# Reordering the filler work of a blocked graph recurrence: last-block tasks after base tasks, VectorE-evicted gates first

## The chip, the cores and the metric

The kernel runs on one core of one Trainium2 chip, in one launch. The metric is the device time of the launch in microseconds. The profile is of one execution whose span is 5644.6 us; times of engines and waits come from it.

## The reference

Four graph layers follow one another on 16 graphs (B) of 1024 nodes (N) with 256 features (D), all in float32. Each layer normalizes, applies ReLU, and adds its result to `x`. Layers 0, 1 and 3 multiply the adjacency matrix with the features. Layer 2, the one that the change touches, is a recurrence over the nodes, in their order:

```python
def step(h, i):
    x = jnp.take(h_e, i, axis=1)
    row = jnp.take(norm_adjT, i, axis=1)
    x_par = jnp.einsum('bj,bjd->bd', row, h)
    iou = x @ W_ioux.T + b_ioux + x_par @ W_iouh.T + b_iouh
    r, z = jnp.split(iou, 2, axis=1)
    r, z = (jax.nn.sigmoid(r), jax.nn.sigmoid(z))
    hc = jnp.tanh(x @ W_coux.T + b_coux + x_par * r @ W_couh.T + b_couh)
    h_new = z * x_par + (1.0 - z) * hc
    h = jax.lax.dynamic_update_slice(h, h_new[:, None, :], (0, i, 0))
    return (h, None)
h_out, _ = jax.lax.scan(step, h_e, jnp.arange(n))
```

A node needs the new rows of those earlier nodes to which it has an edge, and the old rows (`h_e`) of the later ones. About 3% of the edges are there.

## The kernel before

`layers_0_1()`, `layer_2()` and `layer_3()` run one after the other. The rest of this section is about `layer_2()`.

**Blocks and sub-blocks.** The 1024 nodes are 8 blocks (t) of 128, a block is 8 sub-blocks (s) of 16. All 16 graphs go together, in two groups (`G2`) of eight, so that 8 graphs x 16 nodes fill the 128 rows of an instruction. Inside a sub-block the 16 nodes are solved in rounds: three always (`round_`, with `change` ahead of the second and third), and more where a chain of edges inside the sub-block is longer. Whether it is, the program knows from a register: `tc.If(n_more[0][s] > 0)` runs `one_more` (L750), and a loop inside it (L753) runs further ones. The Else arm has no round.

**What enters a sub-block.** The sums over parents come in four parts:

- base tasks (`base_tasks`, L414): for the nodes of the next block, the sums over all rows but those of the block just before them. In block t they work for block t+1 and read the rows of the blocks 0 to t-1 from `hn_d`, the new rows in DRAM, and those from t+1 on from `he_d`, the old ones. A graph's rows are the tile `hb` (two DMAs, L392 and L393), its part of the adjacency is `ab` (L389), masked on GpSimd (L398). A graph takes 7 tasks of two products each, all in one PSUM tile `pf`, which VectorE then scales and writes to `bxt` (L420). `ab` and `hb` have two buffers each.
- last tasks (`last_tasks`, L456): the sums over the rows of the block just before, for all nodes of a block but its first 16. They run in the first sub-block of a block, one task of two products for each graph; the rows are `hr` (L441, from `hn_d`), the adjacency is `ao` (L438), scaled on GpSimd (L452). A pair of graphs shares one `ao` and one `hr`, two buffers each; every task has a `pf` of its own, which VectorE adds to `bxt` (L459).
- far tasks (`far_tasks`, L564): the same inside a block, from one sub-block to the later ones; `next_block` (L551) gives the first 16 nodes of the next block (`pnx`).
- `near` (L772): from a sub-block to the next one.

`pf` has three buffers, shared by base tasks, last tasks, far tasks and gates.

**The order of the work.** TensorE, VectorE, ScalarE and GpSimd are under a manual schedule: their queues are in the order in which the program calls them. A sub-block has a list `todo` of base tasks (14 in each) and of the list `behind`, which is the last tasks in the first sub-block and the far tasks in the others. The two are interleaved, the one with the larger share left going first. The closure `fill(weight)` then issues tasks until the issued cost reaches the given part of the list's cost, at six points of a sub-block: 0.15 ahead of the first round, 0.2 in each of the first two rounds after the pc products (while ScalarE and VectorE finish the round), 0.12 in each `change` after the px products, and the rest in the third round. A task's TensorE work is issued at once, its eviction is put in the list `late` and issued at the next `evict()`.

**Gates.** The input part of the gates for the sub-block ahead is in the class `Gates`: two r tasks (L528, 128x256, evicted by ScalarE at L530) and two z tasks (L536, 128x512, evicted by VectorE at L538). They are four calls in `self.tasks`. In the Else arm they run one after the other, evictions one task behind; in `one_more` they are its fillers: one ahead of the px products, one after them, one after the pc products, the last at the end. `seed_r` (L541) and `seed_zc` (L544, L545) copy the results to the PSUM tiles `pr`, `pc` and `pz`, to which the rounds add.

**DMAs.** Loads are issued by SP, whose queue is ordered by a scheduler by need; a load waits for its buffer there and holds up those behind it. The new rows `h` go out in two stores to `hn_d` from GpSimd's queue (L766) at the end of every sub-block, and only then can `hr` and the rows of the newest block in `hb` be read.

Of the kernel before, what the change touches and what calls it, by code (L numbers as in the profile page):

```python
# [19 lines left out]
DC = D // P  # L20
# [3 lines left out]
G2 = 2  # L24
# [14 lines left out]
def gnn_stack(ctx: ExitStack, tc: tile.TileContext, a: dict, out: bass.AP):  # L39
# [278 lines left out]
    def layer_2():  # L318
        with ExitStack() as st:
# [111 lines left out]
            def last_tasks(t, bxt, dv):  # L431

                n = P - S
                loaded = {}

                def load(b0):
                    ao = big.tile([P, 2, n], F32, name="ao")
                    nc.sync.dma_start(ao, a["adj"][b0 : b0 + 2, (t - 1) * P : t * P, t * P + S : (t + 1) * P]  # L438
                                      .rearrange("b p i -> p b i"))
                    hr = big.tile([P, 2, D], F32, name="hr")  # L440
                    nc.sync.dma_start(hr, hn_d[b0 : b0 + 2, (t - 1) * P : t * P].rearrange("b p d -> p b d"))  # L441
                    loaded[b0] = ao, hr

                def task(b):
                    def run():
                        b0 = b - b % 2
                        if b % 2 == 0:
                            if b == 0:
                                load(0)
                            if b + 2 < B:  # L450
                                load(b + 2)
                            nc.gpsimd.tensor_tensor(loaded[b][0], loaded[b][0], dv[:, b : b + 2, S:], ALU.mult)  # L452
                        ao, hr = loaded[b0]
                        pl = psum.tile([P, DC, n], F32, name="pf", bufs=3)
                        for c in range(DC):
                            nc.tensor.matmul(pl[:, c], hr[:, b - b0, c * P : (c + 1) * P], ao[:, b - b0],  # L456
                                             start=True, stop=True)
                        to = bxt[:, :, b, S:]
                        return lambda: nc.vector.tensor_add(to, to, pl)  # L459
                    return 0.4, run  # L460
                return [task(b) for b in range(B)]

            def load_block(t):
# [14 lines left out]
            class Sub:  # L478
# [3 lines left out]
                def __init__(self, t, s, dp):  # L482
                    self.s, self.dp = s, dp
                    self.n = P - s * S + (S if t + 1 < NT else 0)
                    j0 = t * P + s * S
                    self.aj = big.tile([P, G2, P + S], F32, name="aj")
                    for g in range(G2):
                        nc.sync.dma_start(self.aj[:, g, : self.n], bass.AP(
                            tensor=a["adj"].tensor, offset=a["adj"].offset + g * GB * N * N + j0 * N + j0,
                            ap=[[N * N, GB], [N, S], [1, self.n]]))  # L490
# [21 lines left out]
            class Gates:  # L512
# [3 lines left out]
                def __init__(self, he, s):  # L516
                    self.hs = big.tile([P, DC, G2 * GR], F32, name="hs")
                    for c in range(DC):
                        nc.gpsimd.tensor_copy(self.hs[:, c].rearrange("p (b i) -> p b i", b=B),
                                              he[:, c, :, s * S : (s + 1) * S])  # L520
                    self.gr = big.tile([P, DC, G2 * GR], F32, name="gr")
                    self.gz = big.tile([P, G2, 2 * D], F32, name="gz")
                    self.tasks = [lambda k=k: self.r(k) for k in range(DC)] + [lambda k=k: self.z(k) for k in range(G2)]

                def r(self, e):
                    pg = psum.tile([P, 2 * D], F32, name="pf", bufs=3)
# [144 lines left out]
            with tc.manual_schedule(engines={mybir.EngineType.PE, mybir.EngineType.DVE, mybir.EngineType.Activation, mybir.EngineType.Pool}):  # L671
# [15 lines left out]
                for t in range(NT):  # L687
# [8 lines left out]

                    for s in range(NS):

                        share = [base_todo.popleft() for _ in range(-(-len(base_todo) // (NS - s)))]
                        todo, lists = [], [behind, share]  # L700
                        sizes = [len(x) for x in lists]
                        while any(lists):
                            i = max(range(2), key=lambda i: len(lists[i]) / max(sizes[i], 1))
                            todo.append(lists[i].pop(0))
                        total = sum(cost for cost, _ in todo)
                        spent = part = 0.0
# [61 lines left out]
                        if s + 1 < NS:  # L768
                            near = psum.tile([P, DC, G2 * GR], F32, name="pa")
                            for c in range(DC):  # L770
                                for g in range(G2):
                                    nc.tensor.matmul(near[:, c, g * GR : (g + 1) * GR], h[:, g, c * P : (c + 1) * P],  # L772
                                                     sub.bd[:, g, :, :S], start=True, stop=True)
                            behind = far_tasks(bxt, h, sub)
                        elif t + 1 < NT:
                            next_block(h, sub.bd, 0, False)
                            near = pnx
                            behind = last_tasks(t + 1, bxt_next, dv_next)
                            bxt, he, dv, dp = bxt_next, he_next, dv_next, dp_next
# [145 lines left out]

    layers_0_1()
    layer_2()
    layer_3()

# [48 lines left out]
```

## Time and profile before

| | us |
|---|---|
| time, median of 3 runs | 5647.41 |
| lowest and highest | 5647.23, 5648.99 |
| span of the profiled execution | 5644.6 |
| layers 0 and 1, recurrence, layer 3 | 1449, 2731, 1465 |
| TensorE busy, whole span | 5215.2 (92%) |
| VectorE busy | 2638.4 (47%) |
| GpSimd busy | 1418.8 (25%) |
| ScalarE busy | 1393.6 (25%) |

A line of a profile has the engine (PE is TensorE, DVE is VectorE, ACT is ScalarE, POOL is GpSimd, SP issues loads), the source line, the operation, the tile that it writes and those that it reads, and a count of records. A float32 product shows as two records of TensorE, so a last task is four. "<-" in brackets names what ended the idle time before an instruction. "DVEq" is VectorE's sequencer: the line named with it is a branch. The chain that ended last covers layer 3 alone here (it begins where the recurrence ends), so it says nothing on the change.

The 64 sub-blocks are very regular. A sub-block in the middle of a block without further rounds takes 35 to 38 us and TensorE idles 0.6 of them; one with a further round takes about 7.3 us more. The first sub-blocks of blocks 1 to 7 take 52.8 to 62.3 us, with 10 to 14 us of idle TensorE.

### The profile page before, as it was taken

To read this page: it belongs to the slowest core of one execution; us is meant where nothing else is said; L and a number is where in the kernel's file an instruction comes from. 1 tells how busy PE (TensorE), PEld (TensorE's weight loads), DVE (VectorE), ACT (ScalarE), POOL (GpSimd) and SP (SyncE) were. 2 spreads that over 40 slices of the span, in tenths; PEclk is the share of its full clock that TensorE was granted. 3 is DMA by queue.
4 is the path that set the end of the run, shared out by engine and by line. 5 is a ranking of instruction groups with operands and counts; after the bars stand their busy time and mean duration, and the time that the engine had idled before them with its cause. 6 is when DMAs were issued, how large, how long until landed. Compare 5 with 4: busy or idle time off the path is not lost. (4 is left out here: it accounts for less than half of the span.)

```text
span 5644.6 us, 63144 instructions
## 1 busy us (share of the span) xinstructions
PE 5215.2 (92%) x22975; PEld 3637.5 (64%) x22975; DVE 2638.4 (47%) x6386; ACT 1393.6 (25%) x2970; POOL 1418.8 (25%) x1823
## 2 busy tenths in 40 slices
PE   6999999995799998999889999998869999999999
PEld 3455554553687787878778788787645655556555
DVE  3454444532254555555545455555544343343433
ACT  1221112110122222222222222222223232222322
POOL 2232222220111212212121211212124243342422
PEclk9999999997899999999999999999989999999999
DMA  3322332215623333233143333321032212122210
GB/s 127 117 106 77 119 119 112 92 51 154 194 81 122 86 96 100 72 109 87 55 119 93 115 92 99 105 79 40 10 126 90 92 65 105 53 105 82 75 52 16
DMA packets 471994, 520.25 MB, mean 92 GB/s; under 512 B 49793, under 2 KB 419457, under 8 KB 469377
## 3 DMA queue, kind: packets, MB, share of 16 engines
q1 hardware_dynamic: 445440, 430.75, 23.6%
q0 software_dynamic: 26112, 84.03, 4.1%
q8 instruction: 227, 3.72, 0.3%
q14 instruction: 215, 1.75, 0.1%
HBM read 430.70 MB, written 83.95 MB: 91 GB/s over the span
## 5 line engine op out<-in xcount | busy, mean ns | idle before, releaser
L414 PE MATMUL pf<-ab,hb 128*128 128x128 f32 x3648 | 517.7, 284 | 46.7 <-DMA hb<-he_d 34.4
L414 PEld LDWEIGHTS pf<-ab,hb 128*128 128x128 f32 x3648 | 492.2, 199 | 80.9 <-issue 41.1
L852 PE MATMUL ph<-ag,w 128*128 128x512 f32 x1024 | 480.4, 612 | 34.6 <-DVE hh L856 34.5
L152 PE MATMUL pa<-at,h 128*128 128x512 f32 x1024 | 459.0, 602 | 34.9 <-DVE ag L157 34.9
L837 PE MATMUL pa<-at,h 128*128 128x512 f32 x1024 | 455.1, 595 | 29.6 <-DMA at<-in_adjT 29.6
L152 PE MATMUL pa<-at,q 128*128 128x512 f32 x1024 | 448.4, 594 | 0.0
L890 PE MATMUL po<-w,hh 128*128 128x256 f32 x2048 | 447.7, 379 | 0.0
L890 PEld LDWEIGHTS po<-w,hh 128*128 128x128 f32 x2048 | 387.8, 190 | 59.3 <-issue 7.9
L152 PEld LDWEIGHTS pa<-at,h 128*128 128x128 f32 x1024 | 194.8, 193 | 272.3 <-issue 224.3
L852 PEld LDWEIGHTS ph<-ag,w 128*128 128x128 f32 x1024 | 179.2, 190 | 295.6 <-DVE hh L856 151.5
L837 PEld LDWEIGHTS pa<-at,h 128*128 128x128 f32 x1024 | 194.0, 191 | 261.9 <-issue 259.9
L629 DVE TENSOR_TENSOR r<-r,x 128x256 f32<-128x256 f32 x450 | 187.3, 428 | 336.6 <-ACT r L628 336.6
L152 PEld LDWEIGHTS pa<-at,q 128*128 128x128 f32 x1024 | 191.1, 190 | 237.3 <-issue 237.3
L858 POOL TENSOR_TENSOR ss<-ss,sq 128x512 f32<-128x512 f32 x224 | 305.1, 1362 | 116.0 <-ACT sq L855 111.5
L586 PE MATMUL pr<-dx,wh 128*128 128x256 f32 x1288 | 312.7, 386 | 7.5 <-DVE dx L603 7.4
L744 POOL TENSOR_TENSOR ho<-ho,dh 128x512 f32<-128x512 f32 x64 | 81.2, 1269 | 940.0 <-DVE dh L647 785.0
L628 ACT ACTIVATE r<-pr 128x256 f32<-128x256 f32 x450 | 148.2, 381 | 644.7 <-PE pr L586 600.9
L586 PE MATMUL pz<-wh,dx 128*128 128x256 f32 x1288 | 304.7, 379 | 0.0
L586 PE MATMUL pc<-wh,drx 128*128 128x256 f32 x1288 | 304.5, 379 | 0.0
L157 DVE COPY ag<-pa 128x512 f32<-128x512 f32 x64 | 44.2, 690 | 488.0 <-PE pa L152 488.0
L586 PEld LDWEIGHTS pc<-wh,drx 128*128 128x128 f32 x1288 | 244.6, 190 | 33.6 <-DVE drx L631 0.3
L586 PEld LDWEIGHTS pr<-dx,wh 128*128 128x128 f32 x1288 | 235.8, 193 | 46.8 <-issue 13.6
(170 smaller groups left out, 8480.6 us busy)
## 6 DMA issues: line engine op xcount, KB each, us to landing
at<-in_adjT SPq DMA_DIRECT2D x128, 1024.0 KB
ab<-in_adj SPq DMA_DIRECT2D x128, 512.0 KB
x<-in_x SPq DMA_DIRECT2D x16, 1024.0 KB
x_d<-x POOLq DMA_DIRECT2D x16, 1024.0 KB, 7.9
he_d<-h POOLq DMA_DIRECT2D x16, 1024.0 KB, 7.9
heT_d<-hT POOLq DMA_DIRECT2D x16, 1024.0 KB, 4.2
he<-heT_d SPq DMA_DIRECT2D x16, 1024.0 KB
hb<-he_d SPq DMA_DIRECT2D x16, 1024.0 KB
```

The lines of the kernel that those rows point to most:

```text
L152: nc.tensor.matmul(pa, h[:, mt, c * P : (c + 1) * P], at[:, mt, n0 : n0 + 512], start=mt == 0, stop=mt == NT - 1)
L157: nc.vector.tensor_copy(ag[:, c, n0 : n0 + 512], pa)
L414: nc.tensor.matmul(pb[:, c], hb[:, j, c * P : (c + 1) * P], ab[:, j], start=j == jts[0], stop=j == jts[-1])
L586: nc.tensor.matmul(to, lhsT, rhs, start=False, stop=True, skip_group_check=True)
L628: nc.scalar.activation(r[:, e], pr[:, e], AF.Sigmoid)
L629: nc.vector.tensor_mul(r[:, e], r[:, e], x[:, e])
L744: nc.gpsimd.tensor_tensor(ho, ho, dh, ALU.add)
L837: nc.tensor.matmul(pa, h[b][:, mt, c * P : (c + 1) * P], at[b][:, mt, n0 : n0 + NH], start=mt == 0, stop=mt == NT - 1)
L852: nc.tensor.matmul(ph, w1[:, c, k * P : (k + 1) * P], ag[:, c, n0 : n0 + NH], start=c == 0, stop=c == DC - 1)
L858: nc.gpsimd.tensor_tensor(ss, ss, sq, ALU.add)
L890: nc.tensor.matmul(po, hh[:, c, k * P : (k + 1) * P], w2[:, c], start=c == 0, stop=c == HC - 1)
```

## The change

Three edits, all in the recurrence. The first pair of last tasks is loaded where the list is made, at the end of the block, rather than in the first task. The gates' z tasks come ahead of their r tasks, in the Else arm and in `one_more`. And in the first sub-block of a block (s is 0) the key of the interleaving is 0 for the last tasks and the number of tasks left for the base tasks, so that all base tasks of that sub-block come first and the last tasks follow; in the other sub-blocks the key is as before.

```diff
                         b0 = b - b % 2
                         if b % 2 == 0:
-                            if b == 0:
-                                load(0)
                             if b + 2 < B:
                                 load(b + 2)
...
+                load(0)
                 return [task(b) for b in range(B)]
...
-                    self.tasks = [lambda k=k: self.r(k) for k in range(DC)] + [lambda k=k: self.z(k) for k in range(G2)]
+                    self.tasks = [lambda k=k: self.z(k) for k in range(G2)] + [lambda k=k: self.r(k) for k in range(DC)]
...
                         while any(lists):
-                            i = max(range(2), key=lambda i: len(lists[i]) / max(sizes[i], 1))
+                            i = max(range(2), key=lambda i: len(lists[i]) / max(sizes[i], 1) if s else i * len(lists[i]))
                             todo.append(lists[i].pop(0))
```

## The prediction

> **What bounds the kernel now.** I read the split of the span by stage first, then TensorE's waits in the recurrence, then the timeline of one block boundary. The stages: 1449 us for layers 0 and 1, 2731 us for the recurrence, 1465 us for layer 3. In the recurrence TensorE is busy 2529 of 2731 us, so it bounds it, and the work in its queue is in a fixed order: any idle microsecond on TensorE there is a microsecond of the run. These are its waits in the recurrence, longest first (engine, what waits, for whom: us in total, times, longest):
>
> ```profile
> PE pf L456 <- DMA hr<-hn_d: 44.9, 14, 4.9
> PE pa L772 <- DVEq L752: 20.5, 22, 0.9
> PE pa L599 <- DVE dh L662: 19.4, 17, 4.1
> PE pa L772 <- DVE gz L538: 16.3, 29, 0.6
> PE pf L456 <- DVE bxt L459: 10.3, 13, 1.2
> PE pf L414 <- DMA hb<-hn_d: 10.1, 5, 3.2
> PE pf L456 <- POOL ao L452: 8.7, 13, 2.4
> ```
>
> The reader sees two families. The rows of L456 and L414 belong to the seven block boundaries; the rows of L772 and L599 are short and come with nearly every sub-block. The windows of the first and the third sub-block of block 4 (length, then each engine's busy time, granted clock, DMA share, GB/s) show how special a boundary is:
>
> ```profile
> 2901.50:2956.00 54.50, 42.90 (x245) 37.25 (x246) 22.91 (x56) 10.13 (x24) 14.49 (x22) 0.91 0.50 129
> 2993.80:3031.00 37.20, 36.64 (x206) 30.93 (x205) 20.70 (x48) 10.13 (x24) 8.03 (x13) 1.00 0.28 89
> ```
>
> 54.5 us against 37.2, 11.6 us of it idle and the clock at 0.91. TensorE's timeline at that boundary:
>
> ```profile
> 2899.32 1.16 PE L551 MATMUL pnx<-bd,h 128*128 128x128 f32 x8 [0.84 <-DVEq L752]
> 2905.34 1.17 PE L456 MATMUL pf<-ao,hr 128*128 128x112 f32 x4 [4.86 <-DMA hr<-hn_d]
> 2908.94 1.22 PE L414 MATMUL pf<-ab,hb 128*128 128x128 f32 x4 [2.44 <-DMA hb<-hn_d]
> 2909.95 1.03 PE L456 MATMUL pf<-ao,hr 128*128 128x112 f32 x4
> 2910.78 1.09 PE L414 MATMUL pf<-ab,hb 128*128 128x128 f32 x4
> 2911.66 1.03 PE L456 MATMUL pf<-ao,hr 128*128 128x112 f32 x4
> 2912.49 2.42 PE L586 MATMUL pr<-x,wh 128*128 128x256 f32 x8
> ```
>
> Two waits, not one: the last task (L456) needs hr, the base task (L414) needs hb, and both were read from hn_d just after it was written. A base task needs the newest rows of hn_d too, because base sums for block t+1 leave out block t but take block t-1, which ended at this boundary.
>
> [...] four records take 1.17 us at 2905.34 and 0.60 us at 2919.07. [...] Here the 128 KB stores of hn_d have a median of 2.8 us from issue to landing. [...] so the 0.37 us of an ao issue is no price, and I measure from issue to user. [...]
>
> **The change, part by part.**
>
> *1. Gates: z before r.* The same matmuls, other order. In an Else arm (no further round), near (L772) waits for VectorE to leave the arm, which it does after the last gz eviction: 0.56 us each. With z first, VectorE ends its second gz 0.89 us (0.2 latency, 0.69 eviction) after z; the two r tasks keep TensorE for 1.73 us (3199.72 to 3201.45) meanwhile, so the wait goes to nothing. ScalarE evicts the last r in 0.47 us and seeds pr in 0.60; near (0.87 us) and the first fill (1.9 us) hide that. Gain 29 x 0.56 = 16.3 us. In the If arm (a further round) z is 0.87 us longer than r, so the first task fills more of the wait for dh (L662): six sub-blocks at 0.4 or 0.8 and three of block 7 at 0.87, about 4.6 us outside boundaries. But at its end only r, 1.73 us, stands where z, 3.44 us, stood, and h is ready 2.42 us after the last pc (3865.11 to 3867.53) plus 0.2 of latency: TensorE waits 0.9 us, as now, so the 20.5 us of DVEq stays. The gz evictions move into the 1.35 us in which VectorE awaits the sigmoid: nothing. **-20.9 us.**
>
> *2. The head of a boundary.* Base tasks come first, so the first wait is for hb. hr(0) is still first on SP's queue (its load moves ahead of the turn), then hb(0); hr(2) falls from second place to behind hb(1). So 256 KB less lie ahead of hb(0). In 2905.34 to 2908.94 hr(2) and hb(0), 768 KB, arrived: 213 KB/us, or 1.2 us for 256 KB; at the 330 packets of 1 KB per us that the transfers reach at their fastest, 0.8. I take 1.0. The stores of hn_d wait for VectorE to leave the arm as well: at block 5 the second is issued at 3206.07, 1.19 us after the end of z (3204.88); with z first it is due 0.10 us after the end of r: 1.1 us earlier. In an If arm the figure is 1.0. So pr starts about 2.05 us earlier, with four tasks done instead of five (the fill stops at 0.15 of the list's cost; 0.44 us remain for later): 1.6 x 6 boundaries = 9.7, and 1.05 at block 7, which has no base tasks. The near wait there is contained in this. **-10.7 us.**
>
> *3. The rest of the first sub-block, blocks 1 to 6.* Now the 16 last tasks alternate with 14 base tasks: fills of 5, 6, 4, 6, 4, 6. After: 4, 6, 3 base tasks, then B13 with L0 to L5, then L6 to L8, then L9 to L15. Each last task takes a pf buffer (three, until VectorE adds it), and each pair an ao and hr buffer (two), which are reloaded and then scaled on GpSimd. Block 7, all last tasks already, shows both prices. TensorE first, then GpSimd:
>
> ```profile
> 3895.59 1.49 PE L456 MATMUL pf<-ao,hr 128*128 128x112 f32 x12
> 3897.30 1.41 PE L599 MATMUL pa<-ai,dh 128*128 128x128 f32 x8 [0.22 <-DVE dh L647]
> 3898.55 0.60 PE L456 MATMUL pf<-ao,hr 128*128 128x112 f32 x4
> 3901.53 0.70 PE L456 MATMUL pf<-ao,hr 128*128 128x112 f32 x4 [2.38 <-POOL ao L452]
> ```
>
> ```profile
> 3898.03 1.27 POOL L744 TENSOR_TENSOR ho<-ho,dh 128x512 f32<-128x512 f32 x1 [4.17 <-DVE dh L647]
> 3899.25 0.66 POOL L494 TENSOR_TENSOR aj<-aj,dp 128x224 f32<-128x224 f32 x1
> 3899.99 0.86 POOL L498 TENSOR_TENSOR ai<-aj,before 128x128 f32<-128x128 f32 x2
> 3900.82 0.66 POOL L452 TENSOR_TENSOR ao<-ao,dv 128x224 f32<-128x224 f32 x1
> ```
>
> The multiply waits behind 2.8 us of other GpSimd work, then the task starts. From a pair's release to its successor's start: 0.2 to the issue, 2.7 to 3.5 from issue to multiply (3.1), 0.66 multiply: 4.0 us. A task is 0.44 us. Count from the end of pc. Fourth fill: B13, L0, L1 end at 1.3; L2 waits for a pf, for dh comes at 2.4 and the eviction takes 0.42, so L2 runs from 2.85 and L3 ends at 3.7; L4 needs pair 0 released (1.3) + 4.0, and 0.5 for ab(3), loaded just ahead: 5.8, end 6.7. Seven tasks are 3.1, idle 3.6. Fifth: L4's multiply ends at 5.75, then the 2.8 us and 0.7, so L6 starts near 9.35 where the px matmuls end at 7.55: 1.8; L8 waits 1.0 for the release at 6.7. Sixth: L12 needs L9 (0.44) + 4.0, L14 follows, end 6.2: idle 3.1. Sum 9.5 us. Now: (44.9 - 30.9 at the heads - 0.4 of block 7 + 10.3 - 1.2 + 8.7 - 2.4) / 6 = 4.8. **+4.7 x 6 = +28.2 us.**
>
> *4. Clock.* No row prices it: gaps of 2.5 us at 1821 and of 2.3 in block 3 were followed by an extra half-rate window, gaps of 2.1 and 2.4 were not. Bounds 0 and one window (3.4 us, costing 1.7) for each of two long gaps, 20 us over six boundaries; I take 0.75 window, 7.6, less 3.4 for the two that go: **+4 us.**
>
> Sum: -20.9 - 10.7 + 28.2 + 4 = +0.6 us on the span of 5644.6. The runs' median is 2.8 above that span: **5648**.
>
> **Rivals.** *Faster:* a reload takes 3.6 us (ao issued 3885.18, task at 3888.81), nothing collides with it, the clock holds: 7.8 us of idle instead of 9.5, so +18; head -12; clock -3: -18, 5629. For it: GpSimd and SP are nearly empty there. Against: the wait at 3901.53. *Slower:* the two-deep pair buffers decide. Each run of last tasks beyond two pairs then pays a reload as at the third fill now (ao issued 2919.70, task at 2924.94: 5.2 us). With 4.7 us on average, 11.3 us of idle, +39, and a half-rate window at each boundary, +7: +15.5, 5663; with 5.3 throughout, near 5675. It decides from 11 us of idle per boundary; below 9.2 the change gains. *It does not do what it says:* the order of the built program has base tasks first and last tasks bunched, z before r, so only 2 in 100, at 5647.
>
> **How the numbers follow.** A measurement of this kernel can tell about 0.2%, 11 us. Forecast (within that band) 0.40, and 0.02 for no effect; slower 0.32; faster 0.26. The likeliest case alone spans 5637 to 5659; with the rivals, 5629 to 5668.
>
> **What would show it.** Waits of L772 for gz gone, those for DVEq still near 0.9; the first L414 after a boundary waiting about 6 us and pr starting 2 us sooner; L456 waiting for bxt, POOL and hr some 9.5 us per boundary; first sub-blocks 3 us longer, later ones without a further round 0.56 shorter. If the last tasks wait far less than that, or the clock drops in every first sub-block, I am wrong.

## The result and the profile after

The changed kernel takes 5627.43 us (median of six runs, 5624.07 to 5636.11), the kernel before 5647.32 us beside it (six runs, 5639.15 to 5648.99). The ratio is 0.9971 with a 95% interval of 0.9958 to 0.9984: 0.29% faster, clear of what a measurement of this kernel can tell, and 1.6 us below the range. The profiled execution of the changed kernel is one of the longer ones, with a span of 5634.4 us, 10.2 us less than the profile of before.

First TensorE's waits in the recurrence of the changed kernel (engine, what waits, for whom: us in total, times, longest). Lines have moved: the last task is now L454, its GpSimd multiply L450, its eviction L457, the px products L598.

```profile
PE pf L414 <- DMA hb<-hn_d: 33.0, 6, 6.4
PE pf L454 <- POOL ao L450: 32.2, 17, 3.0
PE pa L772 <- DVEq L752: 16.3, 22, 0.8
PE pa L598 <- DVE dh L661: 11.3, 7, 4.2
PE pf L454 <- DMA hr<-hn_d: 11.3, 7, 4.9
...
PE pf L454 <- issue: 7.8, 6, 1.3
...
PE pf L454 <- DVE bxt L457: 1.6, 2, 1.2
```

Four things have happened among the rows that the prediction shows. The row of near waiting for gz (16.3 us) is gone. The rows for dh (19.4 before) and for the branch, DVEq (20.5 before), have shrunk, the second of which was to stay. The head of a boundary now waits for hb alone, where it waited for hr and hb in turn (block 7, without base tasks, still waits for hr, 4.9 us). And the wait of last tasks for GpSimd's multiply has grown from 8.7 to 32.2 us; whether the two pair buffers are the reason is tested below. A fifth thing is in a row of before that the prediction left out:

```profile
PE pa L772 <- issue: 6.8, 2, 5.0
```

"issue" means that the profile names nothing that the instruction waited for. Near stood still for 4.99 us at the end of the first sub-block of block 1 and for 1.85 us in block 3, and the profile of after has no such row.

The window of the first sub-block of block 4 (columns as in the window shown before) and TensorE's timeline at the same place. A sub-block's window runs from VectorE's first addition of bxt into x (L721) to that of the next sub-block:

```profile
2892.31:2952.07 59.76, 47.59 (x245) 41.30 (x246) 23.75 (x56) 9.31 (x23) 16.16 (x22) 0.83 0.49 136
```

```profile
2890.16 1.16 PE L550 MATMUL pnx<-bd,h 128*128 128x128 f32 x8 [0.65 <-DVEq L752]
2897.37 3.78 PE L414 MATMUL pf<-ab,hb 128*128 128x128 f32 x16 [6.06 <-DMA hb<-hn_d]
2900.95 2.69 PE L585 MATMUL pr<-x,wh 128*128 128x256 f32 x8
...
2918.85 1.04 PE L454 MATMUL pf<-ao,hr 128*128 128x112 f32 x8
2921.20 1.12 PE L454 MATMUL pf<-ao,hr 128*128 128x112 f32 x8 [1.30 <-issue]
2924.31 2.05 PE L454 MATMUL pf<-ao,hr 128*128 128x112 f32 x8 [2.00 <-POOL ao L450]
...
2936.62 1.49 PE L454 MATMUL pf<-ao,hr 128*128 128x112 f32 x12
2941.13 3.76 PE L454 MATMUL pf<-ao,hr 128*128 128x112 f32 x16 [3.02 <-POOL ao L450]
2944.68 4.73 PE L535 MATMUL pf<-wx,hs 128*128 128x512 f32 x8
```

The sub-block takes 59.76 us instead of 54.50, and its idle time is hardly more: 12.2 us (59.76 less 47.59) against 11.6. What is new is the clock, 0.83 against 0.91. The timeline says where: eight records, two last tasks, take 1.04 us at 2918.85 and 2.05 us at 2924.31, and z takes 4.73 us where it takes 3.60 elsewhere. At this boundary the array ran at half rate before for 10.2 us, at the head only (granted clock 0.50 from 2903.28 to 2913.51); now it does so for 6.8 us at the head (0.50 from 2895.73 to 2902.55) and 6.8 us after each of the two longer waits for the multiply (0.50 from 2923.03 to 2929.86 and from 2940.10 to 2946.93).

Summed over the recurrence from the windows of all 64 sub-blocks, in us. Time at half rate is worked out from the granted clock, which in the recurrence is 1 or 0.5 in the traces of before and after: twice (1 - clock) times the length. "Plain" are the 31 other sub-blocks without a further round, "with a round" the 26 others with one; the columns of the first sub-blocks leave out that of block 0.

| profile of | first sub-blocks of blocks 1 to 7: length | idle | at half rate | plain: length | with a round: length |
|---|---|---|---|---|---|
| before | 398.9 | 81.0 | 74.4 | 1102.5 | 1177.9 |
| after | 426.2 | 85.9 | 129.7 | 1071.0 | 1166.8 |
| difference | +27.3 | +4.9 | +55.3 | -31.5 | -11.1 |

So the change gains 42.6 us in the ordinary sub-blocks and loses 27.3 in the seven special ones. That makes -15.3; layers 0 and 1 and layer 3, in which nothing was changed, took 3.0 and 2.1 us longer in this execution, which makes the -10.2 of the span.

### The profile page after: what moved, and what is told of

It is laid out like the page before. It is cut to its first block, busy times and chain, and to the rows that moved or that the text cites. A ratio compares the mean times of both kernels' runs of the same rounds, so it can differ in the third digit from the quotient of the medians.

```text
span 5634.4 us, 63163 instructions
## 1 busy us (share of the span) xinstructions
PE 5231.9 (93%) x22975; PEld 3665.8 (65%) x22975; DVE 2637.1 (47%) x6386; ACT 1395.4 (25%) x2970; POOL 1419.9 (25%) x1823
## 5 line engine op out<-in xcount | busy, mean ns | idle before, releaser
L585 PEld LDWEIGHTS pr<-dx,wh 128*128 128x128 f32 x1288 | 244.5, 197 | 57.5 <-issue 20.5
L535 PE MATMUL pf<-wx,hs 128*128 128x512 f32 x512 | 244.4, 612 | 32.7 <-DMA hb<-he_d 31.1
```

The source lines that it names most:

```text
L535: nc.tensor.matmul(pg, self.hs[:, c, g * GR : (g + 1) * GR], wx[:, c, D:], start=c == 0, stop=c == DC - 1)
L585: nc.tensor.matmul(to, lhsT, rhs, start=False, stop=True, skip_group_check=True)
```

## The experiments

Two readings of the result were open: that the gates gain more than the 21 us of my sum while the order of the tasks costs about what I took or more; or that the gates are worth what I took and the order is what gained. The expectations below, written before each run, name them in their own words. The first four kernels ran beside one another (before: 5652.35 us), then the next four (before: 5646.99), then the last two (before: 5647.59).

### The gates alone

The kernel before, with z ahead of r in `self.tasks` and nothing else.

> The kernel before with one edit: z tasks ahead of r tasks. Theory G (the gates carry the gain, about 0.8 us in a sub-block without a further round and 0.5 in one with it, and the order of the tasks takes part of it back): 40 to 45 us below before, about 5605, and below the changed kernel. Rival P (the size that the prediction gave to the gates, 21 us): about 5626, as the changed kernel, and the order is worth nothing. Rival H (the gain comes from the head of the boundaries): 5640 to 5647.

5588.31 us, ratio 0.9879 (0.9861 to 0.9897): -64 us, three times the 20.9 of my sum. TensorE's waits in its recurrence:

```profile
PE pf L456 <- DMA hr<-hn_d: 35.4, 10, 5.4
PE pa L772 <- DVEq L752: 16.3, 22, 0.8
PE pa L599 <- DVE dh L662: 11.4, 7, 4.2
```

The rows of L772 and L599 are those of the changed kernel, so all that happened to them is the gates' doing. The wait for hr fell as well, from 44.9 to 35.4, but the base tasks waited longer for theirs: from pnx to pr the seven boundaries together take 77.9 us instead of 82.6. That the stores of the new rows go out earlier, because VectorE leaves the arm earlier, fits these 4.7 us and was not tested by itself. In its profile 45.6 us of the gain lie in the ordinary sub-blocks (29.8 plain, 15.8 with a round), and 19.2 in the seven first ones. Of these 19.2, 5.0 are near's wait for "issue" in block 1, which is gone here too.

### The order alone

The changed kernel, with r ahead of z again.

> The changed kernel with the gates back to r ahead of z: base tasks ahead of the last tasks, first pair loaded early. Theory G: 15 to 30 us above before, 5662 to 5677, with TensorE at half rate for about 20 us of a first sub-block. Rival H: below before, by 10 us or more.

5684.92 us, ratio 1.0060 (1.0046 to 1.0074): +33 us. The order of the tasks, with its early load, is a loss. Its first sub-blocks take 427.2 us against 398.9, with 119.5 us at half rate. The second reading falls.

### The gates, one arm at a time

z ahead of r in the Else arm alone, then in `one_more` alone, both on the kernel before:

```diff
-                                for task in gx.tasks:
+                                for task in gx.tasks[DC:] + gx.tasks[:DC]:
```
```diff
-                            one_more(x, rx, h, ho, sub.ai, gx.tasks if gx else ())
+                            one_more(x, rx, h, ho, sub.ai, gx.tasks[DC:] + gx.tasks[:DC] if gx else ())
```

> The kernel before with z ahead of r in the Else arm alone. Theory G: 31 sub-blocks outside the boundaries at 0.8 to 1.0 us and the three boundaries that come out of an Else arm: 30 to 40 us below before. Theory P (0.56 us each, the idle time that the trace shows): 16 to 20 us. Waits of L772 for gz gone, those for DVEq at 20.5 us.

> The kernel before with z ahead of r in the further round (one_more) alone. Theory G: 26 sub-blocks at 0.5 to 1.0 us and four boundaries, 18 to 30 us below before. Theory P: 5 to 10 us (a wait for dh filled in six to nine sub-blocks, the wait of near for VectorE unchanged).

Else alone: 5603.7 us, 0.9916 (0.9903 to 0.9930), -43 us. If alone: 5624.23 us, 0.9952 (0.9938 to 0.9965), -23 us. They add to -66, beside -64 for both. I had 16.3 and 4.6, so Theory P falls in both. The waits of the kernel with the If arm alone changed:

```profile
PE pa L772 <- DVE gz L538: 16.9, 30, 0.6
PE pa L772 <- DVEq L752: 16.3, 22, 0.8
```

The first row, the Else arm's, is nearly as before (16.3). The second is the If arm's: 20.5 before, 20.5 again with the Else arm alone changed, 16.3 here. So that wait did depend on the order of the gates. The "issue" wait of near is 7.7 us with the If arm alone changed and absent with the Else arm alone changed. With r first in the Else arm all three profiles have it (6.8, 7.7, and 3.6 with the order alone), with z first one of nine (3.4, without the early load); what causes it is not known.

### Four pair buffers in the changed kernel

Room for four pairs, three loaded where the list is made:

```diff
-                    ao = big.tile([P, 2, n], F32, name="ao")
+                    ao = big.tile([P, 2, n], F32, name="ao", bufs=4)
...
-                    hr = big.tile([P, 2, D], F32, name="hr")
+                    hr = big.tile([P, 2, D], F32, name="hr", bufs=4)
...
-                            if b + 2 < B:
-                                load(b + 2)
+                            if b + 6 < B:
+                                load(b + 6)
...
-                load(0)
+                for b in (0, 2, 4):
+                    load(b)
```

> The changed kernel with four buffers instead of two for ao and hr, three pairs loaded where the list is made, and each further pair loaded three pairs ahead. If the reload of the two pair buffers makes the waits of the bunched last tasks (7 us of idle in a first sub-block, and the clock windows after them): the waits of L454 for POOL fall from 32 us to under 10 and the time by 15 to 35 us, to about 5600. Rival: the three pf buffers hold the last tasks just as long: waits for bxt take their place, and the time falls by less than 8 us. A second rival: more loads ahead of hb at the head make the first wait longer, and the time does not fall.

5587.03 us, ratio 0.9883 (0.9864 to 0.9902), less than the changed kernel by 40 us by the medians and by 50 us by the ratios, which allow for the different runs of the kernel before beside them. Its waits in the recurrence:

```profile
PE pf L414 <- DMA hb<-hn_d: 48.1, 6, 9.5
...
PE pf L454 <- issue: 15.4, 12, 1.3
```

The wait for the multiply is down to 4.6 us and the time at half rate to 71.7, although the head's wait for hb grew by 15 us; three pairs of hr now stand ahead of it in the queue. The rival is there in part: "issue" has doubled from 7.8 to 15.4 us, and it fits a wait for a pf buffer, since in the changed kernel the task at 2921.20 starts 0.1 us after VectorE ends the eviction that frees one (2920.68, 0.42 us). Even so the bunched order with four buffers takes no longer than the alternating order with two (5588.31 beside it): most of what bunching costs comes from the two-deep pairs.

### Without the early load

The changed kernel with `load(0)` in the first task again, as in the kernel before.

> The changed kernel without its first edit: the first pair of last tasks is loaded by the first last task. If the early load puts hr(0) ahead of hb(0) in the queue of loads and so lengthens the wait at the head by 0.5 to 1.2 us in six boundaries: 3 to 8 us below the changed kernel. If the load in time matters for the first last tasks: 5 to 20 us above it, with a wait of L456 for POOL of 4 us more per first sub-block.

5620.39 us, ratio 0.9947 (0.9934 to 0.9961), against 0.9971 for the changed kernel: about 14 us by the ratios, 7 by the medians, with intervals that overlap a little; probably a small loss by the early load. The profile shows both its sides:

```profile
PE pf L456 <- POOL ao L452: 35.4, 20, 3.0
PE pf L414 <- DMA hb<-hn_d: 27.4, 6, 5.8
```

With hr(0) no longer ahead of hb(0), the head waits 27.4 us instead of 33.0; the last tasks wait 35.4 instead of 32.2.

### No tasks ahead of the first round

At a boundary, the tasks ahead of the first round wait for hb or hr, and that round, which needs neither, waits behind them. So, on the kernel before with z ahead of r, the first fill is moved behind the round's products:

```diff
-                        fill(0.15)
+                        if s or not t:
+                            fill(0.15)
...
-                        rx = round_(x, x, None, None, lambda: fill(0.2), ho)
+                        rx = round_(x, x, None, None, lambda: fill(0.2 if s or not t else 0.35), ho)
```

> The kernel before with z ahead of r, and in the first sub-block of blocks 1 to 7 no task ahead of the first round (its share is given to the fill after the pc products), last and base tasks interleaved as before. The first round needs only pnx and bxt, not hr or hb. If the head's wait of 5 to 7 us is there only because tasks stand in TensorE's queue ahead of work that is ready: some 4 us of idle and a half-rate window go at each of seven boundaries, 35 to 50 us below the gates-only kernel, about 5565. Rival: the loads come too late even then, and the wait moves to the next fill: within 10 us of the gates-only kernel.

5537.94 us, ratio 0.9806 (0.9791 to 0.9820): 50 us less than with the gates alone. The window of the first sub-block of block 2, and the boundary ahead of it on TensorE:

```profile
2136.85:2182.01 45.16, 40.05 (x245) 34.59 (x246) 23.94 (x55) 9.33 (x24) 15.73 (x22) 1.00 0.53 147
```

```profile
2134.58 1.16 PE L551 MATMUL pnx<-bd,h 128*128 128x128 f32 x8 [0.65 <-DVEq L753]
2137.42 1.97 PE L586 MATMUL pr<-x,wh 128*128 128x256 f32 x8 [1.68 <-DVE x L722]
...
2143.23 0.59 PE L456 MATMUL pf<-ao,hr 128*128 128x112 f32 x4
2143.66 0.62 PE L414 MATMUL pf<-ab,hb 128*128 128x128 f32 x4
```

pr starts 2.84 us after pnx, where it took 12.27 us at this boundary with the gates alone (2150.02 to 2162.29). While the round runs, hr and hb arrive, and the tasks find them there. The clock does not fall in this sub-block; the time at half rate in the first sub-blocks of the seven blocks is 10.2 us instead of 58.0 with the gates alone.

### The same head with the changed order, and with deep pairs

The edit of the head on the changed kernel; then the edit of the head on the alternating order with four pair buffers. Both have z ahead of r.

> The changed kernel, all three edits, with no task ahead of the first round of blocks 1 to 7. If bunching the last tasks costs by itself, through reloads and the half-rate windows after them: well above the interleaved kernel with the same free head (5538), by 20 to 40 us, with the waits of L454 for POOL at 25 to 35 us. Rival: the half-rate windows come from the head's wait and not from the bunched tasks; then it is within 10 us of 5538.

> The kernel with z ahead of r and no task ahead of the first round of a block, plus four buffers for ao and hr and three pairs loaded ahead. If the waits left in the first sub-blocks come from the pair buffers (L456 for POOL, hr and issue, 20 us): 10 to 20 us below the kernel without the deeper buffers. Rival: the wait for a pf buffer (10.4 us) and the recurrence's own chain are what is left: within 6 us of it.

On the changed order: 5584.86 us, 0.9891 (0.9875 to 0.9906), still 47 us behind the alternating order with the same head. Its waits and the window of the first sub-block of block 2:

```profile
PE pf L454 <- POOL ao L450: 30.8, 18, 3.1
```
```profile
2144.26:2200.79 56.53, 47.90 (x245) 40.90 (x246) 23.55 (x55) 9.30 (x23) 15.39 (x22) 0.82 0.48 138
```

The head's wait for hb is gone and the clock is still at 0.82: the bunched last tasks, whose waits for the multiply are none above 3.1 us, are enough for that.

With four pair buffers and the alternating order: **5526.34 us**, 0.9787 (0.9774 to 0.9801), 121 us below the kernel before and 2.1% faster. It beats both kernels. Against the same head with two pair buffers it gains 11 us by the ratios, with intervals that overlap, at the low end of what was expected; the wait for the multiply falls from 13.3 to 2.4 us. The window of its first sub-block of block 2:

```profile
2132.11:2174.83 42.72, 39.30 (x245) 34.43 (x246) 24.13 (x55) 9.33 (x24) 16.05 (x22) 1.00 0.60 165
```

### The changed kernel again

Run once more, since the parts didn't seem to add up.

> The changed kernel once more, on the chip of the run above. Theory: the gates' gain (64 us alone) less the order's loss (33 us alone) adds up to 31 us below before. As measured first: 20 us. Below 15 us or above 40 us would say that the parts do not add.

5628.46 us, ratio 0.9971 (0.9959 to 0.9984), the same as the first time. The product of the parts is 0.9879 x 1.0060 = 0.9938, so 0.0033 or 19 us, with an interval of about 15 us each way, of the two parts do not add. The profiles say where: with the old order the gates save 19.2 us in the first sub-blocks (398.9 to 379.7), with the bunched order 1.0 (427.2 to 426.2). The head is still shorter there, but the time at half rate does not fall (119.5 without, 129.7 with z first). How the half-rate stretches fall was not tested by itself, so this stays open. Some of it may be chance: in the two profiles of the changed kernel the first sub-block of block 6 has 20.5 and 13.7 us at half rate.

## Why the prediction was wrong, by its steps

**The step that failed is the first, the gates.** Its mechanism was right: z first takes the gz wait away and fills more of the wait for dh. Its size was not: -20.9 us predicted, -42.6 in the ordinary sub-blocks of the changed kernel (-31.5 where I had 16.3, -11.1 where I had 4.6), and -64 us when made alone. Two terms were mis-sized.

*A wait was priced by the printed idle time.* I took 29 x 0.56 us. The end of an Else arm in block 4 in the trace of before, and another one in block 4 of the trace after:

```profile
3029.04 0.38 PE L772 MATMUL pa<-bd,h 128*128 128x128 f32 x2
3029.99 0.94 PE L772 MATMUL pa<-bd,h 128*128 128x128 f32 x6 [0.56 <-DVE gz L538]
3030.76 0.60 PE L564 MATMUL pf<-bd,h 128*128 128x256 f32 x2
```

```profile
3163.22 1.05 PE L772 MATMUL pa<-bd,h 128*128 128x128 f32 x8
3164.11 1.06 PE L550 MATMUL pnx<-bd,h 128*128 128x128 f32 x8
```

From the start of near to the start of what follows it was 1.72 us before and is 0.89 now: 0.83 us, not 0.56. The printed idle counts only from the end that the profile gives to the two records ahead of the wait, 0.38 us after their start, where two of eight in a row take 0.22 (a quarter of 0.89); so it leaves 0.16 us out, and starts are what should have been subtracted. (A smaller part is that the six records after the wait take 0.77 us, where six of eight in a row take 0.67.) In the middle of blocks 0 to 6 a plain sub-block did become 0.83 us shorter; there are 23 of these. The rest of the 31.5 us goes back mostly to waits that I had left out. In block 7 three sub-blocks became about 1.7 us shorter, where a gates' task had waited for a pf (2.4 us in all before). Three ends of blocks became 1.3 shorter, where pnx had waited for gz (1.7 us in all). One sub-block of block 3 became 3.5 shorter, where near had waited for "issue" and the clock had been lower. Over the 57 ordinary sub-blocks the printed idle time fell by 34.4 us and slower work grew by 4.0, half of the added time at half rate; so 12.2 of the 42.6 us are time that the printing misses.

*The end of the If arm was taken for a standstill.* I had written that r is too short to hide the way to h, so "the 20.5 us of DVEq stays". The If arm of one sub-block in the trace before, and the same place with the gates alone changed:

```profile
1983.66 3.60 PE L536 MATMUL pf<-wx,hs 128*128 128x512 f32 x8
1988.19 1.13 PE L772 MATMUL pa<-bd,h 128*128 128x128 f32 x8 [0.93 <-DVEq L752]
```

```profile
1975.82 1.89 PE L528 MATMUL pf<-hs,wx 128*128 128x256 f32 x8
1978.44 1.13 PE L772 MATMUL pa<-bd,h 128*128 128x128 f32 x8 [0.74 <-DVEq L752]
```

From the last gates' task to near it is 4.53 us before and 2.62 with z first; the task itself is shorter by 1.71 (1.73 in place of 3.44, the durations of the prediction), so 0.20 us were gained at this place, as the printed waits say too (0.93 and 0.74), and the row went from 20.5 to 16.3. The whole sub-block became 0.50 us shorter. The other 0.3 were lost before at the px products between the two r tasks: from the first r task to pr it took 2.94 us, where the two tasks (0.87 each) and px (0.89) make 2.63, and the profile prints no wait there. The row for dh fell by 8.1 us (19.4 to 11.3); I had taken 4.6 there and nothing for the other row. In the changed kernel the sub-blocks with a round gain 11.1 us and not 15.8 because their time at half rate rose, from 27.4 to 39.6 us; with the gates alone it is 29.3.

*A third effect was not in the step at all:* the 19 us that the gates alone save in the first sub-blocks. I had the earlier stores under the head, but not the half-rate time that goes with them (74.4 to 58.0 us with the gates alone), nor near's 5.0 us in block 1; in the changed kernel little of it is seen.

**Step 2, the head: -10.7 us; it holds in the main.** From the near products pnx to pr the boundary of block 4 took 13.17 us before and takes 10.79 now, 2.4 us less; I had 2.05. Over the seven boundaries it is 67.2 us instead of 82.6. Of these 15.4 us, 2.6 are the task that each of six fills leaves for later, so 12.8 stand beside my 10.7. They are not even: 4.0 at block 1, 1.5 to 3.5 at blocks 2 to 6, nothing at block 7, where I had 1.05. The first base task waits 6.06 us at block 4; I expected about 6. One reading of mine was wrong without effect: 330 packets of 1 KB per us is the rate at this boundary and not the fastest, since the trace of before reaches 380 elsewhere.

**Step 3, the rest of the first sub-block: too large.** Idle per boundary was to rise from 4.8 to 9.5 us. It rose to 7.4: (32.2 for the multiply + 11.3 for hr + 7.8 for issue + 1.6 for bxt, less 2.4, 4.9 and 1.2 that belong to block 7) / 6. That makes +15.6 us, not +28.2. The cause is as predicted: each pair beyond the two buffers waits for its reload and its multiply, and with four buffers that wait is 4.6 us in all. At block 4 the idle time ahead of last tasks is 1.30 + 2.00 us in the fourth fill (3.6 in my working), 0.55 in the fifth (1.8, and 1.0 for L8) and 3.02 in the sixth (3.1). The fifth fill is the one that came out too long, and not because its work was ready sooner. L6 starts 9.48 us after the end of pc (2918.41 to 2927.89), where I had 9.35, behind the same GpSimd work. But TensorE was busy until then: L4, L5 and px took 3.58 us at half rate (2924.31 to 2927.89), where at full rate they take 1.76. The 1.8 us of idle time of this step came as slow work, which I counted in the next. (The second fill of before has five tasks and not the six of my list; nothing follows from it.)

The windows of the first sub-blocks show less than +15.6: +4.9 us of idle time, made of -3.3 up to pr and +8.2 after it. After pr other waits of TensorE went at the same time, near's 5.0 us for "issue" and 1.7 for gz.

**Step 4, the clock: far too small.** +4 us predicted. Of the +27.3 us of the first sub-blocks, 4.9 are idle time, so the other 22.4 are slower work. I allowed three quarters of a half-rate window for two gaps per boundary, at 1.7 us a window; 22.4 us over seven boundaries are 3.2 each, and the time at half rate rose by 55.3 us, 7.9 per boundary. The gaps that I compared were also misread: the one of block 3 is 2.60 us and not 2.3; 2.27 is the gap of block 2, and no half-rate window followed it. The windows after the gaps of blocks 1 and 3 are 3.4 us each (granted clock 0.50 from 1824.66 to 1828.08 and from 2531.22 to 2534.64). What the traces show beyond that is in the last section.

Steps 2 to 4 together were +21.5, and the first sub-blocks lost 27.3, with what the gates saved in them included: too much idle time and too little slow work nearly cancel, in part because one turned into the other. With the gates at -42.6 in place of -20.9 and the rest left as it was, the sum would have been 5626. Of the rivals, "faster" named nearly the right time, 5629, for reasons that did not happen: a reload without collisions and a clock that holds. "Slower" had the right mechanism for the tasks, and the order alone does lose 33 us; the gates outweigh it.

## What to carry to other kernels

Price a wait on TensorE by the distance from start to start, with it and without, and not by the idle time that the profile prints; over the 57 ordinary sub-blocks the difference was 12 us of the 42.6. List the small waits too: in the plain sub-blocks those left out here were worth about 6 us. Where work in a fixed queue needs data that has just been written, let work that is ready go first: moving four or five tasks behind one round took 50 us off, more than any order among those tasks. And before consumers of a buffered stream are bunched, compare the reload with what lies between two of them: alternating with other work hid most of it (8.7 us of waits for the multiply before), bunching laid it bare (32.2), and two more buffers took it away (4.6).

## What was not expected of the hardware

Half-rate stretches followed short waits, and more of them than the prediction allowed for. No run was made for this; it is read from the traces of before and after. At block 4 of the changed kernel the granted clock fell after a wait printed at 3.02 us, and after two of 1.30 and 2.00 us with one stretch of work of about a microsecond between them. These are the 3.41 us ahead of each fall and the stretches after them:

```profile
2919.62:2923.03 3.41, 1.39 (x11) 1.06 (x9) 2.81 (x8) 0.00 (x0) 0.00 (x0) 1.00 0.77 220
2923.03:2929.86 6.83, 5.52 (x24) 5.25 (x24) 1.99 (x6) 0.38 (x1) 4.24 (x7) 0.50 0.72 209
2936.69:2940.10 3.41, 1.42 (x13) 1.24 (x11) 2.50 (x7) 0.66 (x2) 0.00 (x0) 1.00 0.38 104
2940.10:2946.93 6.83, 5.80 (x19) 4.59 (x20) 1.55 (x4) 0.00 (x0) 1.32 (x2) 0.50 0.41 103
```

TensorE is busy for 41 and 42% of the first and third line, and in the second and fourth the granted clock is 0.50. The gaps of before had come out both ways: after the wait of 2.51 us in block 1 the clock was 0.50 for 3.4 us, and after the 2.27 us of block 2 it stayed at 1.00 (2176.24 to 2507.33). Two gaps do not settle what decides.

Here slow work cost more than the waits: with the change the first sub-blocks have 4.9 us more idle time, with the shorter head in it, and 22.4 us more of slow work.
